# Two attentions over pairs of positions, rewritten as small parts that run in a written order on four engines

## The chip, the cores and the metric

The kernel runs on one core of a Trainium2 chip. The metric is the time of one execution on the device in microseconds (us). Five engines of the core appear below: PE (TensorE, with its weight loads listed apart as PEld), DVE (VectorE), ACT (ScalarE), POOL (GpSimd) and SP (SyncE, which here only issues DMAs). PE writes to PSUM, of which the pools here take up to 8 banks of 128 x 512 numbers; everything else lies in SBUF.

## The reference

The input `x` has 2 x 1024 tokens of 128 features. Eight residual steps are applied to it in turn: a windowed attention, a mixture-of-experts feed-forward, a causal attention, the feed-forward again, the attention called `a1` here, a six-layer network `ffn1`, the attention called `b1` here, and `ffn1` again. Every step reads a layer norm of `x`. The change touches `a1` and `b1` alone, and both are tiny attentions: the reference takes the batch of 2 as the axis over which it attends, so that at each position a token sees itself and the token at the same position of the other batch.

```python
# a1: 16 heads of 8 features; s and t run over the 2 tokens of a pair
q, k, v = heads(x @ Wq + bq), heads(x @ Wk + bk), heads(x @ Wv + bv)
logits[s, t] = (q[s] . k[t]) / sqrt(8)
gates = sigmoid(logits)                      # summed from the end: a position between 0 and 2
logits += an interpolation, by that position, between q . pos_emb[0], q . pos_emb[1], q . pos_emb[2]
out = softmax_t(logits) @ v
x = x + out @ Wo + bo

# b1: the weights are sums of 4 Kronecker products A (4x4) by S (32x32), for q, k, v and o
qn = layernorm(x) * g1 + b1
q, k, v = relu(qn @ Wq + qb), relu(x @ Wk + kb), x @ Wv + vb
# q and k are multiplied by the sine and the cosine of the token's place; with two places
# this makes w[s, t] = (q[s] . k[t]) * (sin_s sin_t + cos_s cos_t)
attn = (w[s, t] / max(sum_t w[s, t], 1e-6)) @ v + qn
out = layernorm(attn) * g2 + b2
x = x + out @ Wo + ob + out
```

## The kernel before

The residual stream is held as four tiles `xt[0..3]`, each with the 128 features on the partitions and 512 tokens in the free dimension ("a block"); blocks 0 and 1 are the first batch, 2 and 3 the second. A pair of tokens is therefore in blocks 0 and 2, or in blocks 1 and 3.

`Net.norm` makes a layer norm of a block: four PE transposes to tokens on partitions (L120), statistics on DVE (L124, L125), the root on ACT (L134), the reciprocal and the scaling on DVE (L135, L143), four transposes back (L152), and an ACT copy (L155, or L157 with gain and bias).

`attn_a1` runs over the four blocks: a norm; a product for the transposed q (L354) with its bias added on ACT (L356); 4 products with 3 position vectors (L359, copied by ACT, L360); and for each of the 4 groups of 128 tokens one product with the joined q, k, v weights (L363), whose 384 columns DVE writes to `qkv` while it adds the bias (L364). When all 16 groups are in `qkv`, `pair_dots` makes the products q by k of 1024 elements on POOL for each (s, t) (L303) and DVE sums each by head (L306). Then one sigmoid for all dots (L371), 12 DVE steps over 128x256 (L375 to L389), two sigmoids (L391, L392), and `pair_mix`: for each s DVE multiplies the values of t = 0 by their weights, POOL those of t = 1 (L324), and DVE adds the two (L328). At the end every block is transposed (L163), copied by ACT (L397), multiplied by `wo` (L399), and added to `xt` by DVE (L400).

`attn_b1` has the same frame. Its weights are built at the start on POOL (L420, L425) from small loaded factors. Each block has two norms, one after the other (`x`, and `xq` with gain and bias, kept as `qn`); the products are L437 and L438 and the bias is added by DVE (L441). When all are there, one ACT instruction applies the Relu to q and k of all groups (L443). After `pair_dots` come the factors (L448), the sum, maximum, reciprocal and scaling (L450 to L454) and `pair_mix`. At the end each block is transposed to features (L163), added to `qn` (L458), normed by the full norm again (with gain and bias), multiplied by the output weights (L462), and added (DVE, L463, and POOL, L464).

The order of instructions on each engine is made when the program is built: a scheduler orders the instructions of `a1` and `b1` by its own priorities. The stages ahead of them and behind them (`Experts` and `Layers`) put the same instructions into a written order with `tc.manual_schedule(engines=ORDERED)`, where PE, ACT, DVE and POOL each take their instructions in the order in which the program gives them. In both cases an engine's queue is then fixed: an instruction that waits holds up what stands behind it on its engine.

Tiles come from pools. `ps` is a PSUM pool in which each tag has 2 banks unless it says otherwise (`tp` 2, `pj` 3); the first PSUM tile of a stage waits until the stage before has read its last one. SBUF pools of consecutive stages share their addresses in the same way, so the loads that `b1` and `ffn1` issue on SP wait for the end of the stage ahead.

Of the kernel before, what the change touches and what calls it, by code (L numbers as in the profile page):

```python
# [13 lines left out]
ALU = mybir.AluOpType  # L14
# [29 lines left out]
}  # L44


class Net:
# [248 lines left out]
    def pair_dots(self, sb, qkv, key):  # L296

        nc = self.nc
        dots = sb.tile([P, 2, 2, P], F32, tag="dots", name=f"dots_{key}", bufs=1)
        for s in range(2):  # L300
            for t in range(2):
                pd = sb.tile([P, 8, P], F32, tag="pd", name=f"pd_{key}_{s}{t}")
                nc.gpsimd.tensor_tensor(  # L303
                    pd, qkv[:, ts(s, 8), 0:D], qkv[:, ts(t, 8), D : 2 * D], ALU.mult
                )
                nc.vector.tensor_reduce(  # L306
                    dots[:, s, t, :], pd.rearrange("p c (h d) -> p (c h) d", d=DH), AX.X, ALU.add
                )
        return dots

    def pair_mix(self, sb, qkv, weight, key):

        nc = self.nc
        out = sb.tile([P, 16, D], F32, tag="mix", name=f"mix_{key}", bufs=1)

        def split(x):
            return x.rearrange("p c (h d) -> p c h d", d=DH)

        for s in range(2):
            part = sb.tile([P, 8, D], F32, tag="pd", name=f"part_{key}_{s}")  # L320
            dst = out[:, ts(s, 8), :]
            for t, (eng, to) in enumerate(((nc.vector, dst), (nc.gpsimd, part))):
                wt = weight(s, t).rearrange("p (c h) -> p c h", h=HEADS)
                eng.tensor_tensor(  # L324
                    split(to), split(qkv[:, ts(t, 8), 2 * D : 3 * D]),
                    wt[:, :, :, None].to_broadcast([P, 8, HEADS, DH]), ALU.mult,
                )
            nc.vector.tensor_tensor(dst, dst, part, ALU.add)  # L328
        return out

    def attn_a1(self, key):
        nc, tc = self.nc, self.tc
        scale = 1.0 / DH**0.5
        with ExitStack() as ctx:
            cp = ctx.enter_context(tc.tile_pool(name="a1c", bufs=1))
            sb = ctx.enter_context(tc.tile_pool(name="a1s", bufs=2))
            ps = ctx.enter_context(tc.tile_pool(name="a1ps", bufs=2, space=PSUM))
# [9 lines left out]
            )  # L347
            qkv = cp.tile([P, 16, 3 * D], F32, tag="qkv", name="a1qkv")
            li = cp.tile([P, 3, 16, HEADS], F32, tag="li", name="a1li")
            for k in range(NBLK):  # L350
                x = sb.tile([P, 512], F32, tag="xn", name=f"a1xn{k}")
                self.norm(self.xt[k], x, ps, f"{key}_{k}")
                pq = ps.tile([P, 512], F32, tag="pj", name=f"a1pq{k}", bufs=3)
                nc.tensor.matmul(pq, wqkv[:, 0:D], x, start=True, stop=True)  # L354
                qT = sb.tile([P, 512], F32, tag="qT", name=f"a1qT{k}")
                nc.scalar.activation(qT, pq, AF.Identity, bias=bq)  # L356
                pl = ps.tile([P, 4, 3, HEADS], F32, tag="pj", name=f"a1pl{k}", bufs=3)
                for c in range(4):
                    nc.tensor.matmul(pl[:, c], qT[:, ts(c, P)], pe, start=True, stop=True)  # L359
                nc.scalar.copy(li[:, :, ts(k, 4), :], pl.rearrange("p c n h -> p n c h"))  # L360
                for c in range(4):
                    pj = ps.tile([P, 3 * D], F32, tag="pj", name=f"a1pj{k}{c}", bufs=3)
                    nc.tensor.matmul(pj, x[:, ts(c, P)], wqkv, start=True, stop=True)  # L363
                    nc.vector.tensor_tensor(qkv[:, 4 * k + c, :], pj, rows, ALU.add)  # L364
            dots = self.pair_dots(sb, qkv, key)

            def tl(name, n=2):
                return cp.tile([P, n, P], F32, tag=name, name=f"a1{name}")

            gate = cp.tile([P, 2, 2, P], F32, tag="gate", name="a1gate")  # L370
            nc.scalar.activation(gate, dots, AF.Sigmoid, scale=scale)  # L371

            l0, l1, l2 = (li[:, n].rearrange("p (s c) h -> p s (c h)", s=2) for n in range(3))
            d1, d2, pos, over, f0, f1 = (tl(n) for n in ("d1", "d2", "pos", "over", "f0", "f1"))
            nc.vector.tensor_tensor(d1, l1, l0, ALU.subtract)  # L375
            nc.vector.tensor_tensor(d2, l2, l1, ALU.subtract)
            nc.vector.tensor_tensor(pos, gate[:, :, 0, :], gate[:, :, 1, :], ALU.add)
            nc.vector.tensor_scalar(over, pos, -1.0, 0.0, ALU.add, ALU.max)
            nc.vector.tensor_scalar_min(pos, pos, 1.0)
            nc.vector.tensor_tensor(f1, d1, gate[:, :, 1, :], ALU.mult)  # L380
            nc.vector.tensor_tensor(f1, f1, l0, ALU.add)
            nc.vector.tensor_tensor(f0, d1, pos, ALU.mult)
            nc.vector.tensor_tensor(over, d2, over, ALU.mult)
            nc.vector.tensor_tensor(f0, f0, over, ALU.add)
            nc.vector.tensor_tensor(f0, f0, l0, ALU.add)
            for t, f in enumerate((f0, f1)):
                nc.vector.scalar_tensor_tensor(f, dots[:, :, t, :], scale, f, ALU.mult, ALU.add)
# [1076 lines left out]
```

## Time and profile before

| what | value |
|---|---|
| median of 3 runs | 4197.7 us (4184.93 to 4197.97) |
| the profiled execution's own time | 4190.64 us |
| its span, first to last instruction | 4188.8 us |
| mean granted TensorE clock | 0.958 |
| `a1`, from its first transpose to the first transpose of `ffn1` | 651.70 to 720.34 us |
| `b1`, from its first transpose to the first transpose of `ffn1` | 2390.51 to 2506.61 us |

The time of an execution is the span and some 2 us around it. A row of the trace names the source line, the engine, the tile written and the tiles read (buffer numbers left out), the shape, and then busy time and mean duration, or start and duration; what stands behind an arrow is what ended the idle time in front of the instruction. The granted clock is the share of the full TensorE clock that the chip allowed in a stretch.

### The profile page before, as it was taken

What the parts mean: (1) busy time and instruction counts of PE and PEld (TensorE: products, weight loads), DVE (VectorE), ACT (ScalarE), POOL (GpSimd) and SP (SyncE); (2) the same over time, 40 slices, a digit from 0 to 9 for tenths busy, and PEclk for the clock granted to TensorE, in tenths of its full rate; (3) what the DMA queues carried; (4) which work ended last, traced back from release to release, by engine and by line L of the source; (5) the groups of instructions that cost most, each with busy time, mean ns of one, the idle gap of its engine ahead of it and who ended that gap; (6) DMA issues with size and microseconds to landing.
All of it is one profiled execution on the core that took longest, in us unless ns stands there. A gap on an engine that the chain in (4) does not pass through costs nothing.

```text
span 4188.8 us, 156424 instructions
## 1 busy us (share of the span) xinstructions
PE 3932.2 (94%) x67608; PEld 2556.2 (61%) x67608; DVE 3107.2 (74%) x5983; ACT 2401.4 (57%) x4507; POOL 2457.2 (59%) x1578
## 2 busy tenths in 40 slices
PE   7789796899999999999999848999999999999998
PEld 4543533566666666666666525666666666666665
DVE  6843545778878787878878657787887878787886
ACT  3433232676666666666666416766666666666665
POOL 1322022777677776776766217776766777667762
PEclk8789898999999999999999968999999999999999
DMA  1000001223233332232222103232233322323222
GB/s 56 2 1 1 1 0 32 81 71 84 74 76 84 76 85 72 73 90 71 69 66 68 45 16 91 73 84 74 74 84 76 84 73 72 91 68 77 62 67 56
DMA packets 181572, 261.53 MB, mean 62 GB/s; under 512 B 51100, under 2 KB 74264, under 8 KB 180632
## 3 DMA queue, kind: packets, MB, share of 16 engines
q1 hardware_dynamic: 180888, 251.52, 23.4%
q8 instruction: 538, 8.81, 0.9%
q14 instruction: 146, 1.20, 0.1%
HBM read 52.09 MB, written 1.05 MB: 13 GB/s over the span
## 4 chain that ended last, share of the span: by engine, by line
PE 82%; DVE 3%; ACT 1%; POOL 1%; issue 1%; DMA 0%; SPq 0%; ACTq 0%; DVEq 0%; POOLq 0%
PE pj_l L943 16%; PE y_l L1174 9%; PE pv_l L1045 9%; PE tqk_l L163 9%; PE av_l L1142 8%; PE sc_l L1092 6%; PE tpr_l L163 4%; PE to_l L163 4%; PE fg_l L1248 3%; PE fy_l L1284 3%; PE fa_l L1269 3%; PE sc_l L1083 2%; PE f0x_e L760 1%; PE f0h_e L693 1%; PE f0x_e L693 1%
## 5 line engine op out<-in xcount | busy, mean ns | idle before, releaser
L972 DVE TENSOR_TENSOR t_l<-pj_l,rot_l 128x512 f32<-128x512 f32 x1536 | 967.9, 684 | 370.3 <-ACT sq_l L952 357.4
L989 POOL TENSOR_TENSOR raw_l<-t_l,t_l 128x1024 f32<-128x1024 f32 x384 | 908.4, 2366 | 530.2 <-DVE on_l L1150 336.2
L943 PE MATMUL pj_l<-wqkv_l,x_l 128*128 128x512 f32 x1536 | 783.3, 612 | 8.1 <-DVE t_l L972 5.7
L1004 POOL TENSOR_TENSOR raw_l<-raw_l,rn_l 128x1024 f32<-128x1024 f32 x384 | 723.1, 1901 | 95.3 <-ACT rn_l L999 88.3
L952 ACT ACTIVATE sq_l<-pj_l 128x512 f32<-128x512 f32 x768 | 461.7, 603 | 369.4 <-PE pj_l L943 361.4
L978 POOL TENSOR_TENSOR sq_l<-sq_l 128x512 f32<-128x512 f32 x384 | 490.9, 1278 | 310.3 <-ACT sq_l L952 307.1
L163 PE MATMUL tqk_l<-ident_sb,raw_l 128*128 128x128 f32 x3072 | 453.2, 279 | 17.0 <-POOL raw_l L1004 14.7
L163 PEld LDWEIGHTS tqk_l<-ident_sb,raw_l 128*128 128x128 f32 x3072 | 356.9, 142 | 162.4 <-issue 123.4
L1022 ACT COPY qT_l<-tqk_l 128x512 f32<-128x512 f32 x384 | 224.8, 585 | 387.6 <-PE tqk_l L163 387.6
L1045 PE MATMUL pv_l<-wqkv_l,x_l 128*128 128x512 f32 x768 | 415.6, 623 | 5.8 <-DVE ln_xn_fl L1228 5.3
L1174 PE MATMUL y_l<-outT_l,wo_l 128*128 128x128 f32 x3072 | 393.7, 281 | 0.0
L1092 PEld LDWEIGHTS sc_l<-kT_l,qT_l 64*32 64x32 f32 x24576 | 294.9, 105 | 155.0 <-issue 144.4
L1174 PEld LDWEIGHTS y_l<-outT_l,wo_l 128*128 128x128 f32 x3072 | 357.5, 191 | 18.2 <-issue 1.0
L1142 PE MATMUL av_l<-vw_l,pT_l 64*32 64x64 f32 x24576 | 358.9, 224 | 3.7 <-issue 3.6
L943 PEld LDWEIGHTS pj_l<-wqkv_l,x_l 128*128 128x128 f32 x1536 | 255.0, 192 | 171.9 <-issue 106.6
L1054 ACT COPY v_l<-pv_l 128x512 f32<-128x512 f32 x384 | 225.0, 586 | 223.0 <-PE pv_l L1045 202.9
L1142 PEld LDWEIGHTS av_l<-vw_l,pT_l 64*32 64x32 f32 x24576 | 292.9, 105 | 71.9 <-issue 65.7
L1150 DVE TENSOR_TENSOR on_l<-av_l,inv_l 128x512 f32<-128x512 f32 x384 | 247.5, 686 | 120.0 <-PE av_l L1142 119.8
L1092 PE MATMUL sc_l<-kT_l,qT_l 64*32 64x64 f32 x24576 | 329.2, 223 | 0.0
L163 PEld LDWEIGHTS tpr_l<-ident_sb,pr_l 128*128 128x128 f32 x1536 | 188.9, 141 | 152.1 <-issue 116.2
L1102 DVE TENSOR_TENSOR pr_l<-sc_l,mx_l 128x512 f32<-128x512 f32 x384 | 265.6, 692 | 13.2
L1101 DVE TENSOR_REDUCE mx_l<-sc_l 128x8 f32<-128x512 f32 x384 | 261.4, 681 | 3.4 <-PE sc_l L1092 3.4
(344 smaller groups left out, 6158.1 us busy)
## 6 DMA issues: line engine op xcount, KB each, us to landing
vw_l<-v_l SPq DMA_DIRECT2D x3024, 64.0 KB
wqkv_l<-in_Wqkv SPq DMA_DIRECT2D x36, 512.0 KB
rot_l<-in_rotary SPq DMA_DIRECT2D x24, 512.0 KB
wo_l<-in_Wo SPq DMA_DIRECT2D x12, 512.0 KB
w_l<-in_W SPq DMA_DIRECT2D x12, 341.0 KB
f_sb<-in_f SPq DMA_DIRECT2D x1, 1936.0 KB
qks_l<-in_qk_scale SPq DMA_DIRECT2D x12, 128.0 KB
w_l<-in_W SPq DMA_DIRECT2D x12, 128.0 KB
```

What stands on the lines that cost most here:

```text
L163: self.nc.tensor.transpose(tp[:, c, :], src(c), self.ident)
L943: self.nc.tensor.matmul(pj.rearrange("p h d -> p (h d)"), self.x[b][0][:, ts(a, P)], self.w[i]["qkv"][:, ds(INNER * s + 512 * u, 512)], st ...
L952: self.nc.scalar.activation(st["sq", s][:, u], st["pj", s, u], AF.Square)
L972: self.nc.vector.tensor_tensor(to, st["pj", s, u], tabs[:, k, None, ts(w, LD // 2)].to_broadcast(half), ALU.mult)
L978: self.nc.gpsimd.tensor_tensor(sq[:, 0], sq[:, 0], sq[:, 1], ALU.add)
L989: self.nc.gpsimd.tensor_tensor(r.rearrange("p h u d -> p u h d"), st["t1", s], st["t2", s], ALU.add)
L1004: self.nc.gpsimd.tensor_tensor(r, r, st["rn"][:, ts(s, LH), None].to_broadcast([P, LH, LD]), ALU.mult)
L1045: self.nc.tensor.matmul(pj, self.x[b][0][:, ts(a, P)], self.w[i]["qkv"][:, ds(2 * INNER + 512 * r, 512)], start=True, stop=True,)
L1092: nc.tensor.matmul(sc[j][ts(c, 32), hp, :], st["q"][rows, hp, ts(c, 32)], st["k"][rows, hp, ds(32 * c, 64)], start=False, stop=(hp == 7),)
L1102: nc.vector.tensor_tensor(p, st["sc"][j], mx[:, :, None].to_broadcast([P, 8, 64]), ALU.subtract)
L1142: nc.tensor.matmul(av[r][ts(c, 32), q, j, :], st["pT", j][rows, q, ts(c, 32)], st["vw"][rows, c, ts(2 * q + j, LD)], start=True, stop=True,)
L1174: self.nc.tensor.matmul(y[:, 0:P], self.w[i]["o"][:, c, :], st["o"][:, c, :], start=(c == 0), stop=(c == 7))
```

## The change

`a1` and `b1` are rewritten; nothing else of the program differs, and on every engine the rest keeps its order (one POOL clearing of `kT` moves from in front of `b1` to behind it).

- Both are cut into parts with names and run under `tc.manual_schedule`, in the order of the strings `A1_ORDER` and `B1_ORDER`. The digits behind a name are the block, or the block and group, or the half and (s, t).
- The middle is done in two halves of the tokens: half 0 needs blocks 0 and 2 alone, half 1 blocks 1 and 3. So `pd` (POOL) and `rd` (DVE) work on 512 elements, 8 times instead of 4 times, and `gt`, `dl`, `ch`, `sg`, `wz`, `mv`, `pt`, `ad` likewise.
- PSUM: 4 banks for each of the two tags.
- `a1`: in the even groups the bias is a PE product of a row of ones and the bias row, ahead of the q, k, v product, and ACT copies the result; in the odd groups DVE adds it as before.
- `b1`: the bias is such a product in all 16 groups, and ACT evicts each group in two instructions, a Relu of 256 columns and a copy of 128, in place of DVE's addition and the one large Relu.
- `b1`: the second norm takes its statistics from the first norm's tokens-by-partition tile (`stb`) and is scaled by 4 ACT instructions (`xq`) instead of transposing back and forth; the gain and bias by tokens are applied on POOL (`q4`, from a new loaded row `b1_gains`), and `qn` is added by POOL within `pt`. The third norm is taken on `mix` in the same way (`stc`, `sqc`, `ofc`, `xc`), in front of the only transposes of the tail (`To`).
- `b1`: the factors come from a small tile `both`, and `wz` does them in one DVE instruction per half. The bias row is loaded as one partition instead of 128.

```diff
+A1_ORDER = """
+    Tin0 Tin2 sta0 sqa0 x10 sta2 Tin3 Tx0 Tin1 fx0 pj00 sqa2 pj03 sta1 x12 pj01 sta3 Tx2 sqa1 ev00
+    sqa3 ev01 fx2 pj02 pj23 ev02 ev03 pj20 x13 ev23 pj21 pj22 x11 ev20 ev21 ev22 pd000 pq2 rd000
+    pq0 pd001 qT2 pl2 Tx1 qT0 rd001 pd010 pd011 rd011 li2 pl0 fx1 li0 Tx3 pj10 dl0 fx3 rd010 gt0
+    ev10 pj12 ch0 sg0 pj13 ev13 mv2 ev12 mv0 pt0 pj32 ev32 ad0 pj31 pj11 pt2 pj33 ev31 ev11 pj30
+    ev30 pq3 pq1 pd100 ev33 qT3 pl3 ad2 qT1 pl1 rd100 pd111 pd110 rd111 pd101 li3 rd110 li1 rd101
+    To0 dl1 To2 gt1 oT0 ch1 sg1 mv3 oT2 mv1 y0 y2 pt3 pt1 ad3 ad1 fin0 To3 To1 oT3 oT1 y3 y1 fin2
+    fin3 fin1
+"""
+B1_ORDER = """
+    Tin2 sta2 sqa2 x12 Tx2 stb2 fx2 sqb2 off2 Tin0 sta0 xq2 Tin1 Tq2 sta1 fq2 Tin3 q42 sqa0 pj22
+    ev22 x10 pj20 pj21 Tx0 stb0 ev20 sqb0 sqa1 off0 xq0 pj23 x11 fx0 ev23 Tq0 fq0 ev21 Tx1 pj01 q40
+    stb1 sqb1 pj03 fx1 sta3 sqa3 pd011 off1 x13 pj02 xq1 stb3 pj00 ev03 ev01 Tq1 ev02 ev00 q41
+    pd001 pd000 fq1 Tx3 sqb3 pj13 off3 pj10 xq3 pj12 rd011 rd001 rd000 ev10 fx3 ev13 pd010 Tq3 fq3
+    rd010 wz0 pt2 pj11 mv2 mv0 ad2 pt0 stc2 ev11 pj31 ev12 pj32 pj30 pj33 ad0 pd100 ev31 ev32 ev30
+    ev33 sqc2 stc0 pd111 rd100 pd110 ofc2 pd101 xc2 To2 fo2 rd111 rd110 rd101 q43 sqc0 wz1 ofc0 y2
+    mv1 mv3 fin2 xc0 pt1 pt3 ad1 stc1 To0 fo0 y0 ad3 xt2 sqc1 ofc1 stc3 xc1 sqc3 ofc3 fin0 To1 xc3
+    fo1 To3 y1 xt0 fo3 y3 fin1 fin3 xt1 xt3
+"""
...
-    def pair_dots(self, sb, qkv, key):
...
-    def pair_mix(self, sb, qkv, weight, key):
...
     def attn_a1(self, key):
...
-            ps = ctx.enter_context(tc.tile_pool(name="a1ps", bufs=2, space=PSUM))
+            ps = ctx.enter_context(tc.tile_pool(name="a1ps", bufs=4, space=PSUM))
...
+            ones = cp.tile([1, P], F32, tag="ones", name="a1ones")
+            nc.gpsimd.memset(ones, 1.0)
...
-            for k in range(NBLK):
-                x = sb.tile([P, 512], F32, tag="xn", name=f"a1xn{k}")
-                self.norm(self.xt[k], x, ps, f"{key}_{k}")
-                pq = ps.tile([P, 512], F32, tag="pj", name=f"a1pq{k}", bufs=3)
-                nc.tensor.matmul(pq, wqkv[:, 0:D], x, start=True, stop=True)
-                qT = sb.tile([P, 512], F32, tag="qT", name=f"a1qT{k}")
-                nc.scalar.activation(qT, pq, AF.Identity, bias=bq)
-                pl = ps.tile([P, 4, 3, HEADS], F32, tag="pj", name=f"a1pl{k}", bufs=3)
...
-            dots = self.pair_dots(sb, qkv, key)
...
-            mix = self.pair_mix(sb, qkv, lambda s, t: pr[:, t, s, :], key)
...
+            def tl(tag, k, bufs=2, shape=(P, 512)):
+                st[tag, k] = sb.tile(list(shape), F32, tag=tag, name=f"a1{tag}{k}", bufs=bufs)
+                return st[tag, k]
+            def bank(name, tag="tp", shape=(P, 4, P)):
+                st[name] = ps.tile(list(shape), F32, tag=tag, name=f"a1{name}")
+                return st[name]
...
+            def pj(k, c):
+                p, odd = bank(f"pj{k}{c}", "pj", (P, 3 * D)), int(c) % 2
+                if not odd:
+                    nc.tensor.matmul(p, ones, rows[0:1, :], start=True, stop=False)
+                nc.tensor.matmul(p, st["fx", k][:, ts(int(c), P)], wqkv, start=bool(odd), stop=True)
+            def ev(k, c):
+                p, to = st[f"pj{k}{c}"], qkv[:, 4 * int(k) + int(c), :]
+                if int(c) % 2:
+                    nc.vector.tensor_tensor(to, p, rows, ALU.add)
+                else:
+                    nc.scalar.copy(to, p)
+            def pd(h, s, t):
+                rows_s, rows_t = (ds(8 * int(x) + 4 * int(h), 4) for x in (s, t))
+                nc.gpsimd.tensor_tensor(
+                    tl("pd", h + s + t, 3, (P, 4, P)), qkv[:, rows_s, 0:D], qkv[:, rows_t, D : 2 * D],
+                    ALU.mult,
+                )
+            def rd(h, s, t):
+                nc.vector.tensor_reduce(
+                    dots[:, int(h), int(s), int(t), :],
+                    st["pd", h + s + t].rearrange("p c (h d) -> p (c h) d", d=DH), AX.X, ALU.add,
+                )
...
+            def sg(h):
+                i = int(h)
+                nc.scalar.activation(pr[:, i, 0], f0[:, i], AF.Sigmoid)
+                nc.scalar.activation(pr[:, i, 1], f0[:, i], AF.Sigmoid, scale=-1.0)
+            def weighted(eng, to, k, t):
+                h, s = int(k) % 2, int(k) // 2
+                wt = pr[:, h, t, s, :].rearrange("p (c h) -> p c h", h=HEADS)
+                eng.tensor_tensor(
+                    by_head(to), by_head(qkv[:, ds(8 * t + 4 * h, 4), 2 * D :]),
+                    wt[:, :, :, None].to_broadcast([P, 4, HEADS, DH]), ALU.mult,
+                )
...
+            with tc.manual_schedule(engines=ORDERED):
+                for word in A1_ORDER.split():
+                    name = next(n for n in sorted(parts, key=len, reverse=True) if word.startswith(n))
+                    parts[name](*word[len(name):])
...
     def attn_b1(self, key):
...
-            rows = self.load_rows("b1_rows", 3 * D, cp)
+            ps = ctx.enter_context(tc.tile_pool(name="b1ps", bufs=4, space=PSUM))
+            rows = self.load("b1_rows", [1, 3 * D], cp)
+            gains = self.load_rows("b1_gains", 2 * D, cp)
...
+            both = cp.tile([P, 2, 2], F32, tag="both", name="b1both")
+            for s in range(2):
+                for t in range(2):
+                    nc.gpsimd.memset(
+                        both[:, s, t : t + 1], float(sn[s]) * float(sn[t]) + float(cs[s]) * float(cs[t])
+                    )
...
+            def offset(k, n):
+                rs = st["rs", n, k]
+                off = st["off", n, k] = self.small.tile([P, 4], F32, tag=f"ln_of{n}", name=f"b1off{n}{k}")
+                nc.vector.reciprocal(rs, rs)
+                nc.vector.scalar_tensor_tensor(off, st["mv", n, k][:, :, 0], -1.0, rs, ALU.mult, ALU.mult)
+            def scaled(k, n, dst, src):
+                rs, off = st["rs", n, k], st["off", n, k]
+                for c in range(4):
+                    nc.scalar.activation(
+                        dst[:, c, :], src[:, c, :], AF.Identity, bias=off[:, c : c + 1], scale=rs[:, c : c + 1]
+                    )
...
+            def pj(k, c):
+                p, t = bank(f"pj{k}{c}", "pj", (P, 3 * D)), ts(int(c), P)
+                nc.tensor.matmul(p, ones, rows, start=True, stop=False)
+                nc.tensor.matmul(p[:, 0:D], st["fq", k][:, t], wf[:, 0:D], start=False, stop=False)
+                nc.tensor.matmul(p[:, D : 3 * D], st["fx", k][:, t], wf[:, D : 3 * D], start=False, stop=True)
+            def ev(k, c):
+                p, to = st[f"pj{k}{c}"], qkv[:, 4 * int(k) + int(c), :]
+                nc.scalar.activation(to[:, 0 : 2 * D], p[:, 0 : 2 * D], AF.Relu)
+                nc.scalar.copy(to[:, 2 * D :], p[:, 2 * D :])
+            def q4(k):
+                q = tl("q4", k)
+                for n, op in enumerate((ALU.mult, ALU.add)):
+                    nc.gpsimd.tensor_tensor(
+                        q, q if n else st["xq", k], gains[:, None, ts(n, D)].to_broadcast([P, 4, P]), op
+                    )
...
+            def wz(h):
+                d, zh = dots[:, int(h)], z[:, int(h)]
+                nc.vector.tensor_tensor(d, d, both[:, :, :, None].to_broadcast([P, 2, 2, 64]), ALU.mult)
+                nc.vector.tensor_tensor(zh, d[:, :, 0, :], d[:, :, 1, :], ALU.add)
+                nc.vector.tensor_scalar_max(zh, zh, 1e-6)
+                nc.vector.reciprocal(zh, zh)
+                nc.vector.tensor_tensor(d, d, zh[:, :, None, :].to_broadcast([P, 2, 2, 64]), ALU.mult)
...
+            def pt(k):
+                part = tl("part", k, 3)
+                weighted(nc.gpsimd, part, k, 1)
+                nc.gpsimd.tensor_tensor(part, part, st["q4", k], ALU.add)
...
+                "Tin": Tin, "sta": sta, "sqa": lambda k: root(k, 0), "x1": x1,
+                "stb": lambda k: moments(k, 1, st["x1", k]), "sqb": lambda k: root(k, 1),
+                "off": lambda k: offset(k, 1), "xq": lambda k: scaled(k, 1, tl("xq", k), st["x1", k]),
+                "Tx": lambda k: flip(f"tx{k}", st["x1", k]), "fx": lambda k: features("fx", k, st[f"tx{k}"]),
+                "Tq": lambda k: flip(f"tq{k}", st["xq", k]),
+                "fq": lambda k: features("fq", k, st[f"tq{k}"], col[:, 0:1], col[:, 1:2]),
+                "pj": pj, "ev": ev, "q4": q4, "pd": pd, "rd": rd, "wz": wz,
+                "mv": lambda k: weighted(nc.vector, block(k), k, 0), "pt": pt,
+                "ad": lambda k: nc.vector.tensor_tensor(block(k), block(k), st["part", k], ALU.add),
+                "stc": lambda k: moments(k, 2, block(k)), "sqc": lambda k: root(k, 2),
+                "ofc": lambda k: offset(k, 2), "xc": lambda k: scaled(k, 2, block(k), block(k)),
...
```

## The prediction

> **What bounds the kernel now.** I read the page first. PE is busy for 94% of the span, and the slices show where it is not: early, and in the slices where `a1` and `b1` lie (the seventh, and the 23rd and 24th), where the granted clock falls too.
>
> ```profile
> span 4188.8 us, 156424 instructions
> PE 3932.2 (94%) x67608; PEld 2556.2 (61%) x67608; DVE 3107.2 (74%) x5983; ACT 2401.4 (57%) x4507; POOL 2457.2 (59%) x1578
> PE   7789796899999999999999848999999999999998
> PEclk8789898999999999999999968999999999999999
> ```
>
> The stages run one after another, so a stage's length is what it is worth. Busy time by stretch (columns: length, busy us and instructions of PE, PEld, DVE, ACT and POOL, granted clock, DMA):
>
> ```profile
> 651.70:720.30 68.60, 38.29 (x128) 21.43 (x128) 40.26 (x94) 13.60 (x25) 16.73 (x9) 0.75 0.00 0
> 689.70:703.30 13.60, 0.00 (x0) 0.00 (x0) 7.78 (x15) 1.04 (x3) 6.94 (x3) 0.61 0.00 0
> 2390.50:2506.60 116.10, 55.58 (x184) 35.14 (x184) 65.47 (x199) 15.74 (x25) 26.54 (x16) 0.64 0.02 5
> 2452.10:2462.50 10.40, 0.00 (x0) 0.00 (x0) 4.77 (x4) 0.00 (x0) 9.24 (x4) 0.50 0.00 0
> ```
>
> The first and third rows are the whole stages: 68.6 and 116.1 us, in which no engine is busy for more than 60%. Four engines together are busy for 108.9 us of `a1` and 163.3 us of `b1`, so 1.59 and 1.41 engines work at a time. In the second and fourth rows PE does nothing. The waits within the two stages say for whom:
>
> ```profile
> POOL pd_e L303 <- DVE a1qkv L364: 34.0, 2, 17.3
> PE a1to L163 <- DVE mix_e L328: 21.3, 1, 21.3
> POOL pd_l L303 <- ACT b1qkv L443: 47.7, 1, 47.7
> PE b1to L163 <- DVE mix_l L328: 25.7, 1, 25.7
> ```
>
> POOL stands until all of `qkv` is there, then PE stands until all of `mix` is there. That is latency, and the halves and the interleaved order go against it. Three groups give the prices that decide (from the timeline, and from the tile view of `mix` as min/median/max ns):
>
> ```profile
> 667.19 2.81 PE L363 MATMUL a1pj<-a_sb,a1xn 128*128 128x384 f32 x8
> 683.62 5.45 PE L363 MATMUL a1pj<-a_sb,a1xn 128*128 128x384 f32 x8
> 703.69 5.60 POOL L324 TENSOR_TENSOR part_e<-a1qkv,a1pr 128x1024 f32<-128x1024 f32 x2 [7.00 <-ACT a1pr L392]
> L324 DVE TENSOR_TENSOR mix_e<-a1qkv,a1pr x2: 1225/2104/2983, 703.3 to 704.5; 128x1024 f32<-128x1024 f32 x2
> ```
>
> The same four products take 2.81 or 5.45 us by the clock: 0.64 or 1.28 us for 384 columns. And a DVE step with two SBUF inputs takes 1.22 us when POOL is idle at its start and 2.98 beside a running POOL step. Per 512 elements I use 0.67 and 1.57.
>
> **Prices.** PE at full clock: 4 transposes 0.43, 384 columns 0.64, 512 columns 0.86, the eight small passes for the position logits 0.95; the double at half clock; 0.25 more until a reader starts. The added product of the row of ones shows in no row; it is priced like its neighbour of 384 columns, 0.64 or 1.28 (it is at least 0, at most the cold value). DVE: statistics of a block 1.62, by the strictly alternating ones at 2373.11 to 2374.73; scaling 1.6 with its reciprocal; head sums of 512 elements 0.66 (half of L306); the 12 steps of `ch` 3.4 (before 4.2 on twice the width, where dependent ones started every 0.46 us); `wz` 2.5 (L450 to L454, halved where the width is). ACT: copy of a block 0.59, with two column operands 0.78, table load 1.28. The four ACT steps of `xq` and `xc` are 0.46 each by the slope between 192 and 512 columns, less 0.1 overlap: 1.56 a block. One group's eviction is 0.44 in `a1` and 0.58 in `b1`. POOL: 512 elements 1.26 (L464), with broadcast weights 1.4.
>
> **`a1`, along its queues.** From the first transpose: transposes, root and DVE's four statistics and two scalings, 10.8 us. `fx2` stands behind `sqa3` on ACT though its input is there: 0.9 (11.7). PE: four groups of block 2 (two with a ones product) 3.8, `pq2` and its bias 1.9, then `pl2`, `Tx1`, `pl0`, `Tx3` 2.8 (20.2). `fx3`, table load, `gt0` 2.5 (22.7). `ch0`, `sg0` 4.0 (26.7). `ev12` is queued behind `sg0` and frees the bank for `pj11`; behind it come `pj33` and `pj30` at half clock, and `ev30`: 6.3 (33.0); DVE's `mv2` to `ev11` lies beside it. Three `pd` of half 1, 3.8 (36.9). `rd101`, `dl1`, `ch1`, `sg1` 5.2 (42.1). `mv3`, `mv1`, `ad3` beside POOL 3.9 (45.9). `To3`, `oT3`, `y3`, `y1` at half clock and `fin1` 6.2: 52.2 us, against 68.6. Saved: 16.4.
>
> **`b1`.** The weights come first, as before: SP issues five loads instead of four, 0.45 more, then seven POOL steps; the first product starts at 14.5 (before: 14.0). The norms of block 2 are hidden under that. Two groups at half clock 5.1, then ACT's queue: `ev20`, `sqb0`, `xq0`, `fx0`, `ev23`, `fq0`, 5.2 (24.8); all of PE waits for it. Four groups and the last eviction 6.0 (30.8). Three `pd` 3.8, `rd010`, `wz0` 3.3 (37.9). DVE: `mv2`, `mv0`, `ad2`, `stc2`, `ad0`, `stc0`, where `mv` and `ad` have two inputs and lie beside POOL, 9.7 (47.6). Meanwhile `pd101` waits for the buffer that `rd100` frees, with `q43`, `pt1` and `pt3` queued behind it; it is done before DVE asks. Four sums, two offsets, `wz1` 6.8 (54.4). `mv1`, `mv3`, `fin2`, `ad1`, `stc1`, `ad3`, `ofc1`, `stc3` 9.8 (64.2). `sqc3`, `ofc3`, `xc3`, `fo1`, two products at half clock, `fin3` 7.7: 71.9 us, against 116.1. Saved: 44.2. Removed with it: 3.6 us of the large Relu, during which all else stood, and twelve of the block transposes of the second and third norms (one of two and two of three in each block). Added and hidden: ACT goes from 16 to 34 us and POOL from 27 to 36, both below DVE's 55; if that cover went, `q4` (10 us) and `xq` (6 us) would be what shows. The `kT` clearing moved behind `b1` (0.3 us on POOL) and the last `xt` steps lie under the first norm of `ffn1`, which takes 7 to 8 us before its first product needs weights (720.34 to 727.05 and 2506.61 to 2514.89); the five small POOL memsets lie under the loads.
>
> **Sum.** 16.4 + 44.2 = 60.6 off the profiled execution's own 4190.6: 4130 us. That execution lies 7 us below the median of the runs shown and within their 13 us, and I take no more out of that. About 0.3% (12.6 us) is what a measurement of this kernel can tell from no change.
>
> Unknown terms between their ends: with PE at full clock throughout and no slow DVE step, `a1` is 47.1 and `b1` 63.1; with PE at half clock throughout and every slow DVE step, 67.9 and 88.0. I stand near the lower ends since the products come in runs, like those at 667, and only the first and last run of a stage begins after idle time, like that at 683.
>
> The rule that bears on this: the granted clock was 1.00 from 664 to 679, with PE 77% busy, but the products at 683.62 stayed slow for 5.4 us of unbroken work. [...]
>
> **Rivals.** (1) PE stays at half clock, since each new wait in its written order cuts the runs short: 155.9 for both stages, 4162 us. For it: mean clocks of 0.75 and 0.64 now. Against it: the idle stretches of 20 and 26 us go. (2) DVE and POOL do not slow each other much and PE is fast: 110.2, 4116 us. Against it: the 2.98. (3) Slower: the written orders block. An engine whose head waits holds what is ready behind it, where the scheduler before could choose. The new work by the prices above is 114 us (40 PE, 43 DVE, 15 ACT, 16 POOL) and 169 us (44, 55, 34, 36), together 283, so it is slower than before as soon as fewer than 283/184.7 = 1.53 engines work at a time; at the 1.41 of `b1` before, it is 201 us, 4207 us. For it: `fx2` behind `sqa3` and the like are in the order. Against it: my walk gives 2.2 and 2.4, and the orders start the other half's work in every wait. (4) The gain is nearly lost in this way, at 1.44 to 1.64 engines: no difference. That the change saves something that was hidden anyway is excluded, since nothing of `ffn1` runs in these stretches.
>
> **How the numbers follow.** Forecast 0.75, (1) 0.11, (2) 0.08, (3) 0.03, (4) 0.03. Faster: 0.94. The range runs from 4112, below (2) by some run-to-run spread, to 4156, towards (1) but without it.
>
> **What would show it.** `a1` near 52 and `b1` near 72 us, between the same transposes; `pd` of half 0 on POOL while products of half 1 run on PE; no PE gap over 6 us after the first product of `b1`; DVE as the engine most busy in `b1`; `mv` and `ad` at 0.7 or 1.6 us; the rest of the span unchanged within 5 us. Wrong would be: PE idle over 15 us in a stage, the ones products above 1.3 us, ACT as the last to end in `b1`, or `ffn1` with another length.

## The result, and the profile after

The changed kernel takes 4138.1 us in the median of 4 runs (4124.7 to 4140.5), where the kernel before takes 4191.3 us in the 4 runs beside it: a ratio of 0.987, 95% interval 0.9842 to 0.9899. The forecast of 4130 us had the direction right and was 8 us too low, within its range. The profiled execution, from which all stage lengths of the changed kernel are read, is the slowest of the four: it took 4140.45 us, 50.1 us less than the one before, where the prediction's sum was 60.6.

The page's header and its row of the granted clock in 40 slices:

```profile
span 4138.7 us, 156507 instructions
PEclk8689898999999999999999969999999999999999
```

The 24th slice, in which `b1` lies, is still the only late one below 9. Busy time by stretch (length, busy us and instructions of PE, PEld, DVE, ACT and POOL, granted clock, DMA): all of `a1`, all of `b1`, and then three parts of `b1`:

```profile
649.90:702.00 52.10, 42.70 (x145) 20.79 (x145) 39.66 (x108) 17.26 (x36) 18.09 (x17) 0.87 0.00 1
2372.30:2454.50 82.20, 64.33 (x168) 32.22 (x168) 53.36 (x164) 32.29 (x88) 43.47 (x39) 0.61 0.02 6
2386.30:2400.30 14.00, 14.00 (x35) 8.23 (x36) 5.12 (x26) 5.40 (x17) 4.98 (x5) 0.50 0.00 0
2400.30:2414.30 14.00, 14.00 (x33) 7.12 (x32) 3.85 (x15) 5.46 (x18) 4.99 (x5) 0.50 0.00 0
2414.30:2428.30 14.00, 14.00 (x52) 7.03 (x52) 12.09 (x23) 6.62 (x21) 9.53 (x8) 0.99 0.01 2
```

`a1` is 52.1 us (forecast 52.2, before 68.6) and `b1` 82.2 us (forecast 71.9, before 116.1). The rest is unchanged within 2 us: the first `ffn1` takes 1670.3 us (before 1670.2), the second 1684.2 to the end of the span (before 1682.2). So nearly all of that execution's miss is in `b1`, and the last three rows show where: from 2386.3 to 2414.3 PE was busy without a pause, and yet at half clock; in the third row the same kind of work runs at full clock. The waits of the two stages that answer to those shown of before (total, times, longest):

```profile
POOL a1pd L429 <- ACT a1qkv L423: 14.0, 2, 10.1
PE a1to L368 <- DVE a1mix L501: 0.9, 1, 0.9
POOL b1pd L646 <- ACT b1qkv L630: 11.7, 3, 7.2
PE b1to L597 <- ACT b1mix L590: 8.9, 4, 3.6
```

POOL's 34.0 and 47.7 us are down to 14.0 and 11.7, PE's 21.3 and 25.7 to 0.9 and 8.9. The waits went as the change meant. What came in their place is seen in PE's own rows of `b1` (start, duration):

```profile
2409.34 1.64 PE L624 MATMUL b1pj<-b_rows_sb,b1ones 1*128 1x384 f32 x2
2410.91 0.80 PE L625 MATMUL b1pj<-b1w,b1fq 128*128 128x128 f32 x2
2411.50 1.06 PE L626 MATMUL b1pj<-b1w,b1fx 128*128 128x256 f32 x2
2412.35 1.06 PE L597 MATMUL b1tq<-ident_sb,b1xq 128*128 128x128 f32 x4
2413.20 1.06 PE L597 MATMUL b1tx<-ident_sb,b1x 128*128 128x128 f32 x4
...
2416.01 0.91 PE L624 MATMUL b1pj<-b_rows_sb,b1ones 1*128 1x384 f32 x2
2416.85 0.49 PE L625 MATMUL b1pj<-b1w,b1fq 128*128 128x128 f32 x2
```

A group is a product of one row, then 128 and 256 columns of 128 rows. From one group to the next it is 3.15 us at half clock (2406.18 to 2409.33) and 1.69 at full clock (2416.01 to 2417.70). Without a gap PE had worked since 2386.3, and the clock came back at 2414.5, 0.3 us behind a stretch of 3.3 us that held no product of one row (2410.91 to 2414.20). An equal stretch from 2396.59 to 2399.88 had not brought it back; what set the two apart was not shown. The clock's own changes here lie at 2373.5, 2414.5 and 2431.6. Theory A, which the experiments test, is a guess from the 28.2 us of unbroken work at 0.50: a product that feeds one of 128 rows does not count as work for the clock.

### The profile page after: what moved, and what is told of

Read it like the earlier page. It is cut to its first block, busy times and chain, and to the rows that moved or that the text cites. A ratio compares the mean times of both kernels' runs of the same rounds, so it can differ in the third digit from the quotient of the medians.

```text
span 4138.7 us, 156507 instructions
## 1 busy us (share of the span) xinstructions
PE 3946.1 (95%) x67608; PEld 2552.9 (62%) x67608; DVE 3090.8 (75%) x5962; ACT 2421.3 (59%) x4581; POOL 2475.3 (60%) x1608
## 4 chain that ended last, share of the span: by engine, by line
PE 82%; DVE 3%; ACT 1%; issue 1%; POOL 1%; DMA 0%; SPq 0%; POOLq 0%; DVEq 0%; ACTq 0%
PE pj_l L1187 16%; PE y_l L1418 9%; PE pv_l L1289 9%; PE tqk_l L185 9%; PE av_l L1386 8%; PE sc_l L1336 7%; PE tpr_l L185 4%; PE to_l L185 4%; PE fg_l L1492 3%; PE fy_l L1528 3%; PE fa_l L1513 3%; PE sc_l L1327 2%; PE f0x_e L1004 1%; PE f0h_e L937 1%; DVE t_l L1216 1%
## 5 line engine op out<-in xcount | busy, mean ns | idle before, releaser
L185 PE MATMUL tqk_l<-ident_sb,raw_l 128*128 128x128 f32 x3072 | 452.4, 278 | 17.2 <-POOL raw_l L1248 14.1
```

Source lines behind the costliest of these rows:

```text
L185: self.nc.tensor.transpose(tp[:, c, :], src(c), self.ident)
```

## The experiments

Stage lengths and clocks are read as above, from one execution of each kernel; times of the kernel are medians of 4 or 5 executions, and ratios are to the kernel before. The executions of one kernel differ: one of the four of the changed kernel took 4124.7 us, as little as the best below, at a mean granted clock of 0.968 where the other three had 0.963 and 0.964, and its trace is not there to say why.

**One row, 128 rows, or none.** The bias product of `b1` with all rows fed:

```diff
-            rows = self.load("b1_rows", [1, 3 * D], cp)
-            ones = cp.tile([1, P], F32, tag="ones", name="b1ones")
-            nc.gpsimd.memset(ones, 1.0)
+            rows = self.load_rows("b1_rows", 3 * D, cp)
+            ones = cp.tile([P, P], F32, tag="ones", name="b1ones")
+            nc.gpsimd.memset(ones, 1.0 / P)
```

> b1's bias product takes 128 rows (the bias on every row, weights 1/128) where it took one row; the same count of instructions and columns. In the changed kernel PE was busy without a gap from 2387.8 to 2414.5 us and yet at a granted clock of 0.50; b1 took 82.2 us where 71.9 were forecast. Theory A (a product of one row does not count as work for the clock, and a stretch that is half made of such products stays slow): the clock goes to 1.00 within 3 to 7 us of the first product, a group of products takes 1.5 us and not 3.15, b1 is 68 to 72 us, the kernel 10 to 14 us below the changed one (about 4126). Rival B (the clock is slow for a fixed time after the idle start of the stage, or for small products whatever their rows): slow until about 2410 again, b1 79 to 82 us, at most 3 us below the changed kernel.

Measured: `b1` 70.3 us, the kernel 4127.6 us (ratio 0.984, 0.9823 to 0.9856). All of `b1`, and the stretch from 3 us behind its first product to the end of the products:

```profile
2366.50:2436.80 70.30, 45.56 (x168) 27.65 (x168) 53.37 (x164) 31.51 (x88) 43.78 (x39) 0.76 0.03 10
2384.50:2406.50 22.00, 21.87 (x111) 16.21 (x110) 16.88 (x51) 16.05 (x51) 13.18 (x11) 1.00 0.00 1
```

The same number of products now ends in PE's 45.6 busy us instead of 64.3, and a group takes 1.30 us. Theory A holds in clock, group and stage. In the medians the kernel is 10.5 us faster than the changed one, as expected, though the two intervals of the ratio still overlap by 0.0014.

The second run takes the product out (the flags of the other two follow), so that q, k and v lack their bias:

```diff
-                nc.tensor.matmul(p, ones, rows, start=True, stop=False)
```

> Leaves out b1's bias product, so q, k and v of b1 lack their bias; all else as in the changed kernel. Theory A: no product of one row is left, the clock goes to 1.00 within 7 us of the first product, a group takes 0.85 us, b1 is 66 to 70 us. Rival B: the clock stays at 0.50 for some 25 us after the first product, a group takes 1.6 us; b1 70 to 74 us from the work that is left out alone.

Measured: `b1` 68.6 us, 4128.7 us. The clock came back 17.2 us after the start of the stage, 3.4 us behind the first product, and fell again from 27.5 to 30.9, after pauses of PE. The gain over the 128-row form is 1.7 us in `b1` and none in the medians: the bias product as such costs little, once it feeds all rows.

**The clock alone.** Six extra products ahead of the first group of `b1`, which still has its one-row bias products. In the first run they feed 128 rows, in the second one row (R stands for 128 or 1):

```diff
+                for _ in range(6 if (k, c) == ("2", "2") else 0):
+                    nc.tensor.matmul(p, self.ident[0:R, :], self.xt[2][0:R, 0 : 3 * D], start=True, stop=True)
                 nc.tensor.matmul(p, ones, rows, start=True, stop=False)
```

> Six extra products (128 rows, 384 columns, their output overwritten) on PE ahead of b1's first group, at 2383.3, mostly while PE waits for the weights. One-row bias products as in the changed kernel. At half clock they take 7.7 us, so the first group starts up to 4.7 us late. Theory A: they release the clock, the groups that follow take 1.69 and not 3.15 us, b1 is 73 to 77 us, the kernel 5 to 9 us below the changed one. Rival B: groups stay at 3.15 us, b1 86 to 88 us, the kernel 4 to 6 us above the changed one.

> The same six extra products in the same place with one row instead of 128. Theory A: PE is as busy, but the clock is not released: the six take 9.4 us, groups stay at 3.15 us, b1 is 86 to 90 us, the kernel 5 to 7 us above the changed one and 12 or more above the 128-row form. Rival B: no difference from the 128-row form beyond 2 us.

Measured: 4132.0 us (0.985, 0.9834 to 0.9867) and `b1` 72.7 with 128 rows, 4150.8 us (0.9893, 0.9862 to 0.9925) and `b1` 100.7 with one row. The traced execution with one row took 4168.6 us, the slowest of its four, so the 100.7 is the extreme and not the usual length. Of each, all of `b1` and one stretch behind the extra products:

```profile
2373.00:2445.70 72.70, 56.23 (x181) 28.53 (x181) 52.36 (x164) 31.85 (x88) 43.42 (x40) 0.74 0.03 7
2388.00:2408.00 20.00, 20.00 (x82) 10.75 (x80) 10.35 (x43) 11.97 (x37) 10.44 (x10) 1.00 0.00 0
```

```profile
2379.80:2480.50 100.70, 83.96 (x181) 41.35 (x181) 53.70 (x164) 32.29 (x88) 43.51 (x39) 0.51 0.02 5
2400.00:2415.00 15.00, 15.00 (x37) 8.33 (x36) 5.14 (x25) 6.12 (x19) 3.29 (x3) 0.50 0.00 0
```

The two kernels differ only in how many rows six products feed. With 128 rows the clock is released and the one-row groups behind them keep it, at 100% busy; with one row it stayed at 0.50 for 99.0 us, from 1.6 us behind the start of the stage to its end, worse than I expected of theory A (86 to 90). So in these runs the one-row products did not bring the clock back, but they did not lose it either (1.00 from 2388.0 to 2408.0 with 128 rows ahead): in the changed kernel too it stays at 1.00 through the second eight groups (2414.5 to 2431.6). Rival B is out.

**What of the rows counts.** Again 128 rows, but the weights are zero in all rows except the first:

```diff
-            nc.gpsimd.memset(ones, 1.0 / P)
+            nc.gpsimd.memset(ones, 0.0)
+            nc.gpsimd.memset(ones[0:1, :], 1.0)
```

> As the run with a bias product of 128 rows (b1 70.3 us), but 127 of the 128 rows of its weights are zero and the first is one, so that the same one row does the work. If what releases the clock is that all rows are fed: released within 8 us of the first product, a group at 1.30 us, b1 69 to 73 us. If it is the arithmetic that is not zero (power): groups stay at 2.56 us for some 25 us, b1 78 to 82 us.

Measured: `b1` 70.7 us, 4130.3 us (0.9844, 0.9829 to 0.9858); the clock came back 20.6 us after the start of the stage, 6.0 behind the first product. So here the rows that are fed count (one row 42.2 us after the start, 128 rows 18.0), not the arithmetic in them. Then 32 rows:

```diff
-            rows = self.load("b1_rows", [1, 3 * D], cp)
-            ones = cp.tile([1, P], F32, tag="ones", name="b1ones")
+            rows = self.load("b1_rows", [32, 3 * D], cp, self.t["b1_rows"].partition_broadcast(32))
+            ones = cp.tile([32, P], F32, tag="ones", name="b1ones")
```

> The changed kernel with b1's bias product on 32 rows (weights 1/32) where it had one and an earlier run had 128. If rows are counted by their share (the stretch of products is then fed to 60 to 65%): the clock stays at 0.50 until a stretch without bias products, b1 79 to 83 us as with one row. If any group of rows is enough: released within 8 us of the first product, b1 70 to 73 us as with 128 rows.

Measured: the profiled execution, the fastest of its four, lies between the two, `b1` 75.7 us with the clock back for the products 28.2 us after the start of the stage (one row 42.2, 128 rows 18.0). It came back 14.3 us behind the first product, after 14.0 us at 0.50 in which PE was busy without a pause (2380.5 to 2394.5). The median is 4139.6 us (0.9872, 0.9845 to 0.9899), no better than one row. So products of 32 rows in the groups were not enough here. Whether a product of 32 rows counts by its share or not at all, and how many rows would be enough, stays open.

**The interleaving.** From the 128-row form, only the order strings are changed: the same words, sorted so that each queue does first all products and evictions, then all `pd` and `rd`, and so on.

```diff
 B1_ORDER = """
...
+    ev32 ev30 ev33 q43 pd011 pd001 pd000 rd011 rd001 rd000 pd010 rd010 wz0 pd100 pd111 rd100
+    pd110 pd101 rd111 rd110 rd101 wz1 pt2 mv2 mv0 ad2 pt0 ad0 mv1 mv3 pt1 pt3
+    ad1 ad3 stc2 sqc2 stc0 ofc2 xc2 To2 fo2 sqc0 ofc0 y2 fin2 xc0 stc1 To0
```

> As the run with a bias product of 128 rows (a1 52.1, b1 70.3 us), with only the written orders changed: in a1 and b1 each queue does all products and evictions first, then all pd and head sums, then the weights, then all mv, pt and ad, then the rest; the halves stay as sizes but are no longer interleaved. Theory (the interleaving carries a good part of the gain, since every engine's wait is filled with the other half): a1 60 to 66 us, b1 75 to 82 us, the kernel 13 to 24 us above that run. Rival (smaller steps and fewer of them carry it, the queues fill the waits in any order): a1 52 to 55, b1 70 to 73 us, at most 6 us above.

Measured: `a1` 58.6, `b1` 81.3, 4146.5 us (0.9884, 0.9869 to 0.9899). The waits of PE for its last transposes, first of `a1` and then of `b1`:

```profile
PE a1to L371 <- DVE a1mix L504: 14.8, 1, 14.8
PE b1to L600 <- ACT b1mix L593: 26.2, 3, 24.6
```

These are the long waits of the kernel before again. The interleaving is worth 6.5 us in `a1` and 11.0 us in `b1`, 17.5 us of the two stages; theory and rival split here, since the smaller and fewer steps alone keep the other 10.0 us of `a1` and 34.8 us of `b1` (all with the 128-row bias in `b1`).

**The bias back on DVE.** One part of the change to `b1` is undone: the product of the row of ones is left out, and DVE adds the bias while it evicts:

```diff
-                nc.scalar.activation(to[:, 0 : 2 * D], p[:, 0 : 2 * D], AF.Relu)
-                nc.scalar.copy(to[:, 2 * D :], p[:, 2 * D :])
+                nc.vector.tensor_tensor(to, p, rows, ALU.add)
+                nc.scalar.activation(to[:, 0 : 2 * D], to[:, 0 : 2 * D], AF.Relu)
```

> Takes back one part of the change in b1: the bias is added by DVE while it evicts (0.55 us a group of 384 columns), ACT then does the Relu in place on 256 columns; no bias product. All else as in the changed kernel (b1 82.2 us). Theory A: no one-row product is left, so the clock is released within 7 us of the first product and a group takes 0.65 us of PE; DVE stands idle for 60% of the product phase, so its 8.8 us are mostly hidden: b1 64 to 70 us, the kernel 12 to 18 us below the changed one. Rival: DVE's adds stand in its queue before statistics that the next block needs, and ACT waits for them: b1 72 to 78 us.

Measured: `b1` 77.4 us, 4135.1 us (0.9855, 0.9839 to 0.9872). The rival's mechanism was right:

```profile
ACT b1qkv L630 <- DVE b1qkv L629: 22.0, 7, 8.3
PE b1pj L624 <- DVE b1qkv L629: 6.7, 1, 6.7
```

ACT and PE wait for additions that stand in DVE's queue, and after each pause the clock was down again (0.50 from 22.2 to 29.0, from 32.4 to 39.2 and from 46.1 us on, counted from the start of the stage). Half of it, odd groups on DVE and even groups by a 128-row product, was tried on the kernel of the next paragraph:

> From the same run (b1 66.7 us): in b1 the odd groups take their bias from DVE while it evicts, as a1 does, with ACT's Relu in place, the even groups from the product of 128 rows. PE has eight products of 0.65 us less, DVE eight additions of 0.55 us more. If PE sets the time of the product stretch and DVE's free time takes the additions: b1 62 to 65 us. If DVE's additions block what stands behind them in its queue, as in the run with all bias on DVE (77.4): 67 to 72 us.

Measured: `b1` 72.9 us, 4134.4 us, 6.2 us more in `b1` than without. ACT waited 9.5 us for DVE's additions, and the clock was lost from 28.2 to 35.0 and from 41.8 to 48.7 us. In this written order the bias belongs on PE, with all rows; what another place in DVE's order would give was not tried.

**The clock held to the end.** Both stages with 128-row bias products, and extra products where PE waits:

```diff
+            def warm(out, n, src):
+                for _ in range(n):
+                    nc.tensor.matmul(out, self.ident, src, start=True, stop=True)
...
                 tp = bank(name)
+                warm(tp[:, 0:3, :], {'tx2': 2, 'tq2': 1, 'pj22': 2, 'to2': 12, 'to0': 2, 'to1': 3, 'y2': 1, 'y0': 1, 'y1': 1}.get(name, 0), wf[:, 0 : 3 * D] if name[0:2] == "to" else self.xt[2][:, 0 : 3 * D])
```

> From the run with a bias product of 128 rows in b1 (a1 52.1, b1 70.3 us): the same in a1, and extra products of 128 rows whose output is overwritten, placed where PE stands idle: five of 384 columns before b1's first group, 19 and some small ones before and between its last transposes and products, nine in a1's tail. Theory A: the clock stays at 1.00 to the end of both stages, the last products take 0.95 and not 1.89 us: a1 48 to 51 us, b1 65 to 69 us, the kernel 4 to 9 us below that run. Rival: the extra products stand before work that is on the path and give back what the clock brings: a1 52 to 54, b1 70 to 73 us.

Measured: 4124.7 us (0.9832, 0.9817 to 0.9847), `a1` and `b1`:

```profile
643.90:695.50 51.60, 43.04 (x186) 26.23 (x186) 39.68 (x108) 17.26 (x36) 18.11 (x16) 1.00 0.00 1
2369.90:2436.60 66.70, 55.93 (x242) 36.67 (x242) 53.94 (x164) 31.44 (x88) 43.42 (x39) 0.97 0.03 10
```

`b1` came as expected, 3.6 us shorter than with 128 rows alone; `a1` gained only 0.5 us, against the 1.1 to 4.1 expected, and the kernel 2.9 us in the medians, against 4 to 9. In `a1` the clock was at 1.00 throughout, so either PE's clock sets little of what is left of it, or the extra products take back what it gives; the run does not separate the two.

**DVE beside POOL.** In half 1 of `b1` the steps of POOL in `pt` go to DVE:

```diff
-                weighted(nc.gpsimd, part, k, 1)
-                nc.gpsimd.tensor_tensor(part, part, st["q4", k], ALU.add)
+                eng = nc.vector if int(k) % 2 else nc.gpsimd
+                weighted(eng, part, k, 1)
+                eng.tensor_tensor(part, part, st["q4", k], ALU.add)
```

> From the run with extra products in the idle stretches (b1 66.7 us): in b1's second half the part products and the addition of q move from POOL to DVE, so POOL does nothing beside DVE's eight steps with two SBUF inputs of 512 elements. If such a step is slow because POOL runs beside it, as the prediction priced it: 0.65 to 0.75 us each, 5.4 us in all for what now takes DVE 5.4 and a wait for POOL, b1 65 to 67 us. If the slowness comes from the operands themselves: 1.2 to 1.7 us each, b1 71 to 74 us.

Measured: `b1` 68.7 us (2.0 more than without, between the two ranges), 4133.0 us. From the timeline of half 1:

```profile
2426.88 0.68 DVE L684 TENSOR_TENSOR b1part<-b1qkv,b1dots 128x512 f32<-128x512 f32 x1
2427.05 1.64 POOL L705 TENSOR_TENSOR xt<-xt,b1fo 128x512 f32<-128x512 f32 x1 [4.55 <-DVE b1fo L702]
2427.60 1.64 DVE L693 TENSOR_TENSOR b1part<-b1part,b1q 128x512 f32<-128x512 f32 x1
2429.94 0.69 DVE L693 TENSOR_TENSOR b1part<-b1part,b1q 128x512 f32<-128x512 f32 x1
```

The same line on the same shape takes 0.69 us alone and 1.64 beside a POOL step that was running when it began; the row at 2426.88 began before POOL and stayed at 0.68. So the slow price of the prediction is shown, but it is no fixed one: the slow step ends 0.55 us after the POOL step (2429.24 and 2428.69), and so does every other slow one of this size in `b1` of the changed kernel, so what it costs is what is left of the POOL step. The move does not pay. From the first `mv` to the last `ad` it takes 8.5 us where it was 7.6, since POOL's two steps a block had lain beside DVE and now stand in its queue; the other 1.1 us lie behind that, where PE's wait for its last transposes was 3.3 us and not 2.4 and the clock was at 0.50 from 2436.3 to 2439.7.

**One word of the order.**

```diff
-    stb1 sqb1 pj03 fx1 sta3 sqa3 pd011 off1 x13 pj02 xq1 stb3 pj00 ev03 ev01 Tq1 ev02 ev00 q41
-    pd001 pd000 fq1 Tx3 sqb3 pj13 off3 pj10 xq3 pj12 rd011 rd001 rd000 ev10 fx3 ev13 pd010 Tq3 fq3
+    stb1 sqb1 pj03 fx1 sta3 sqa3 pd011 off1 x13 pj02 xq1 stb3 pj00 ev03 ev01 Tq1 ev02 ev00
+    pd001 pd000 fq1 Tx3 sqb3 pj13 off3 pj10 xq3 pj12 rd011 rd001 rd000 ev10 fx3 ev13 pd010 q41 Tq3 fq3
```

> The run with extra products in the idle stretches (a1 51.6, b1 66.7 us, 4124.7 us), with one word of b1's order moved: q4 of block 1, two POOL steps of 1.27 us which half 1 alone needs, stands behind the third pd of half 0 instead of ahead of the first, where in the run with a 128-row bias the first pd began 0.93 us after its input was there. If half 0's chain through POOL sets the time: head sums, wz0 and all behind them 0.9 us earlier, b1 65.5 to 66.0 us. If DVE's queue sets it: b1 unchanged at 66.5 to 67. The kernel 4119 to 4126 us, 0.982 to 0.984 of the kernel before.

Measured: 4124.7 us (0.9834, 0.9821 to 0.9848), `b1` 67.3. The first head sum began 1.1 us earlier in the stage (27.8 against 28.9 us) and `mv` no earlier (34.8 against 34.7). Neither rival had the place: the two steps of `wz0` in this run, then the same steps in the run with extra products, and POOL in this run:

```profile
2403.86 0.76 DVE L675 TENSOR_TENSOR b1dots<-b1dots,b1both 128x256 f32<-128x256 f32 x1
2404.66 1.24 DVE L676 TENSOR_TENSOR b1z<-b1dots 128x128 f32<-128x128 f32 x1
```

```profile
2402.06 0.43 DVE L675 TENSOR_TENSOR b1dots<-b1dots,b1both 128x256 f32<-128x256 f32 x1
2402.52 0.29 DVE L676 TENSOR_TENSOR b1z<-b1dots 128x128 f32<-128x128 f32 x1
```

```profile
2403.07 1.26 POOL L655 TENSOR_TENSOR b1q<-b1xq,b_gains_sb 128x512 f32<-128x512 f32 x1
2404.42 1.33 POOL L655 TENSOR_TENSOR b1q<-b1q,b_gains_sb 128x512 f32<-128x512 f32 x1
```

POOL, moved out of the way of the first `pd`, now ran beside `wz0` and slowed its two steps by 1.3 us (they end 0.29 and 0.15 us after the POOL step beside them): the gain was paid back by the price that the run above had shown. Both kernels of 4124.7 us have ratios below the changed kernel's 0.987, and the intervals overlap by 0.0006 at most.

## Why the prediction was nearly right

**`a1`: right, with two errors that cancel.** The forecast and measured ends, in us from the first transpose: `fx2` 11.7 and 11.5, `gt0` 22.7 and 23.3, `sg0` 26.7 and 27.1, `ev30` 33.0 and 30.9, the last `pd` 36.9 and 37.1, `sg1` 42.1 and 42.1, `fin1` 52.2 and 52.0. `pj33` and `pj30` ran at full clock, 2.1 us earlier than forecast, but then not three but four `pd` stood in a row on POOL (5.4 us from 681.62, forecast 3.8), because `pd100` waited for DVE's last additions.

**`b1`: one term was mis-sized, its first run of products.** The same ends with the two kernels that differ in that term:

| end of | forecast | changed kernel | 128-row bias |
|---|---|---|---|
| `ev00`, last eviction of half 0 | 30.8 | 40.8 | 28.8 |
| `wz0` | 37.9 | 48.4 | 36.7 |
| `stc0` | 47.6 | 57.9 | 46.2 |
| `wz1` | 54.4 | 64.7 | 53.0 |
| `stc3` | 64.2 | 74.4 | 62.7 |
| `fin3` | 71.9 | 82.1 | 70.3 |

The error is 10.0 us at the first line and 10.2 at the last: each of the five sums behind the first line was right within 0.5 us. (POOL was busy for 43.5 us of `b1` and not 36, since the 36 leave out the 7.9 us in which it builds the weights; that stayed hidden.) The mis-sized term is "two groups at half clock 5.1, then ACT's queue ... 5.2; four groups and the last eviction 6.0". All eight groups of half 0 ran at half clock, and each took 3.15 us where I had 2.55. The one-row product costs more than the 0.64 or 1.28 us of its neighbour: 0.84 us from its start to the next product at full clock and 1.57 at half; and the two products behind it take 1.58 us at half clock and not 1.28. ACT's queue, the wait I named, never held PE up. With the 128-row bias the same walk is right within 2 us all the way, though there too ACT's queue did not hold PE up.

Behind that term stood the weighing of the clock rows. I read the 5.4 us of slow unbroken work in `a1` before as a late release and took runs of products as what brings the clock back. The clock of that trace was at 0.50 from 682.4 to 689.2, 6.8 us in which PE was busy for 6.67, all of it on products of 128 rows: most of eight small ones of 48 columns, then those at 683.62. So there the clock did come back behind 6.8 us of nearly unbroken work. In `b1` of the changed kernel the 28.2 us of unbroken work from 2386.3 to 2414.5 stood at 0.50, so that PE had something to do was not enough. They fit if a one-row product is no work for the clock, as in the two runs with six extra products: 1.00 behind those of 128 rows, 0.50 for 99.0 us with those of one row. How long a run of 128-row products has to be was not shown.

**The other signs.** Held: `pd` of half 0 beside products of half 1, no PE gap over 6 us in `b1` (the longest is 3.6), `mv` at 0.7 or 1.6 to 1.7, `ffn1` unchanged within 2 us, and the table load in its new place took 1.28 us with `gt0` 0.01 us behind it (671.50). In `b1` `mv` and `ad` are, as min/median/max ns:

```profile
L667 DVE TENSOR_TENSOR b1mix<-b1qkv,b1dots x4: 691/1566/1746, 2420.7 to 2438.7; 128x512 f32<-128x512 f32 x4
L698 DVE TENSOR_TENSOR b1mix<-b1mix,b1part x4: 896/1252/1547, 2424.1 to 2443.6; 128x512 f32<-128x512 f32 x4
```

Failed: `ad` lies mostly between the two prices (0.90, twice 1.25, 1.55), by what was left of the POOL step beside it. The shortest, with 0.35 us left of that step, ends 0.55 us after it:

```profile
2439.90 1.52 POOL L667 TENSOR_TENSOR b1part<-b1qkv,b1dots 128x512 f32<-128x512 f32 x1
2441.07 0.90 DVE L698 TENSOR_TENSOR b1mix<-b1mix,b1part 128x512 f32<-128x512 f32 x1
```

Also, DVE is not the busiest in `b1` (53.4 us against PE's 64.3), and the ones products are above 1.3 us (1.57 at half clock). The prediction had named the latter as a sign of being wrong, and it was the right one to name. Rival (1), PE at half clock, came true for 28 us of `b1`, but not for its reason: no wait cut the runs short. Rival (3), blocking orders, did not come in the changed kernel (2.3 engines work at a time in `a1`, 2.4 in `b1`: PE, DVE, ACT and POOL are busy for 117.7 us in 52.1 and 193.5 in 82.2), but is what the runs with DVE's additions in the old order show.

## What to carry to other kernels

Read the granted clock beside PE's busy share: a stretch that is 100% busy and at 0.50, as the 28.2 us of `b1` here, asks which products feed few rows, and a product padded to all rows can then be cheaper than a small one (here 0.65 us with 128 rows and 0.84 with one, both at full clock). In a written order an operation that moves to another queue holds up what stands behind it there, as DVE's additions did (22.0 us of ACT's waits). And a walk along the queues sized by rows of the trace held within half a microsecond over most of its sums; its weak term was the one new operation for which no row existed.

## What the runs showed of the hardware

- The TensorE clock stayed at 0.50 through 28.2 us of unbroken work of `b1`, some 40% of it one-row products, and came back 0.3 us behind 3.3 us without them; an equal 3.3 us earlier in that stretch had not brought it back. With six more one-row products ahead it stayed at 0.50 for 99.0 us of the stage, with six of 128 rows it was at 1.00 in the stretch from 15.0 to 35.0 us behind the start of the stage. Rows that are fed against zero weights count (clock back 6.0 us behind the first product). Once back, the clock stayed at 1.00 through one-row groups (2414.5 to 2431.6 in the changed kernel, the last group ending at 2428.3).
- A one-row product of 384 columns takes 0.84 us to the next product, one of 128 rows 0.65, and the two products behind it take 0.85 instead of 0.65 us at full clock. With 32 rows the records of such a product lie between the same ends as with one row, 0.481 and 1.004 us against 0.481 and 1.005 (128 rows 0.486 and 0.847). Why such a product slows its successors was not tried.
- A DVE step with two SBUF inputs of 512 elements takes 0.68 us alone and 1.64 beside a POOL step that runs at its start; one of 128 elements 0.29 and 1.24, one of 256 elements 0.42 and 0.76. The slow steps end 0.55, 0.15 and 0.29 us after the POOL step, so the loss is what is left of that step, less some 0.14 us, and it hits POOL too: the POOL step at 2427.05, begun beside a running DVE step, took 1.64 us where its like takes 1.26.
- The executions of the run with six one-row products spread from 4136.9 to 4168.6 us, more than of any other kernel here. That the release depends on where stretches without one-row products happen to fall would explain it; it was not shown.
